# A four-layer graph network on one core: one closing branch, and the order of some loads, sums, turns and copies

## The chip, the core and the metric

The kernel runs on one core of a Trainium2 chip. A core has five engines, each with its own queue that is worked off in order: TensorE (PE, matmuls and transposes; the profile shows the loading of weights beside it as PEld), VectorE (DVE), ScalarE (ACT), GpSimd (POOL) and SyncE (SP), which here issues most of the transfers between the chip's memory (HBM) and the on-chip memory. Engines wait for each other through semaphores. The metric is the device time of the core in microseconds (us); less is better.

## What is computed

The input is x (3327 rows of 256 numbers, float32) and a square matrix adj of 3327 rows. Four layers follow; each normalises x by rows, cuts at zero (h), and adds something to x:

```
# layers 0, 1 and 2
h = relu(layernorm(x));  x = x + adj @ (h @ W0.T + b0)
h = relu(layernorm(x));  x = x + relu(new_adj @ (tanh(h @ Wp + bp) @ Wg) + bg)
#   new_adj: tanh(adj*adj), the 700 largest of each row (all that are positive, if fewer)
h = relu(layernorm(x));  x = x + relu(A_norm @ (h @ W2.T))
#   A_norm: adj + 1, scaled on both sides by 1/sqrt of its row sums
# layer 3
h = relu(layernorm(x));  R = (adj + 1) / row sums;  Xf = Xa = h;  Z = 0
for n in range(2):
    logits = (Xa @ W1.T @ W2.T) @ (Xa @ W3.T).T
    A  = softmax(logits), in each row only the largest up to a mass of 0.9, renormalised
    Xf = R @ Xf;  Xa = A @ Xa
    Z  = Z + Xf @ U1[n].T + Xa @ U2[n].T
x = x + layernorm(h + Z) * ln_g + ln_b
```

The result is x after the four layers, 3327 x 256.

## The kernel before

**Tiling.** The 3327 rows are padded to 26 blocks of 128 (T = 26 in the code, H = 13 the half). All products are in float32. A large product of 26 x 26 blocks is split in 2 x 2 quarters and done with seven products of quarters instead of eight, with sums of quarters made by VectorE. So the blocks are worked off in pairs p and p + 13, and one pair takes 91 matmuls of 128 x 128 with 128 columns, each of which is two records in the profile.

**Layers 0 to 2** (`layers_0_to_2`). `products` (L592) goes over the 13 pairs of a layer; a `Feed` loads the pieces of adj on SP, VectorE and ScalarE make the sums of quarters and the tanh. While a pair's products run, the pair before it is finished, and what the next layer needs of its rows is done by a `Pair`: normalise (`normed`, L359), turn by transposes (L391), project. The stages of a Pair are hooked between the products at counts that the table `WHERE` gives, one entry for each number of stages; with two stages it is layer 1, at the 54th and 82nd product of a pair. The very first rows are loaded and worked on by `first_two` (L737), which has no products to lie behind. In `normed`, VectorE makes mean and variance of two blocks, POOL the inverse root (L98 and L100), and VectorE or ScalarE applies it (L379 and L375).

**Layer 3** (`layer_3_in`, L886). It has two steps. For each of the 26 rows of blocks, TensorE makes the logits (L970), ScalarE their exps (L995), and a search on ScalarE and VectorE (`search_steps`, L999 to L1077) finds the row's threshold and zeroes what is below: it begins with ScalarE's L1012 to L1017 and a pass over the whole row on ScalarE (L1028) and VectorE (L1031), and its last pass over the row (L1073) leaves e, the attention before its division. The search runs AHEAD = 3 rows in front. Then TensorE turns e by blocks (L186), ScalarE copies the turned blocks (L189), and TensorE multiplies them with the values (L197). In between, a `PropagatedPair` (L1149) does R @ Xf, in two phases, with slabs of adj or of its sums; the unit matrix is added to a slab's diagonal block by POOL (L1163). A slab is asked for at the first unit that uses it, and its buffers rotate. `combine` (L1136) makes the sums of quarters on VectorE (L1141 to L1144). `AttentionOfFirstStep` has three parts, `turn`, `node` and `values`; `PropagationOfFirstStep` has `scale`, `turn` and `sums`. `finish3` (L1286) ends a row: it loads z (kept from step 1) and x, adds, normalises, and its `store` writes the result.

**What sets the order.** TensorE's order is the program's, written out by hand: generators yield after each unit, and a plan `{unit: [actions]}` tells what is done at which unit (`run`, L127). On the other engines a scheduler sets the order at build time; `tc.high_priority()` moves an operation forward, and `tc.issue_after(op)` keeps it behind another in its queue. SP's and ScalarE's transfers stand in the queues of their engines with the rest.

**The checks.** The search for a threshold can fail to settle for a row, and a layer-1 row can have more than 700 positive entries. Both are counted, and if it happens the rows, or all layers, are done again by slower code. For this the program reads a flag into a register on all engines and branches (`if_failed`, L1414, with the reads and branches at L1418 and L1419): once in the middle of layer 3, between the two steps, once at the end for step 2, and then once more for all layers (L1740). With this data no branch is taken:

```
        if_failed(0, flags0, st0, kT0, redo_first, lambda name: first_e, redo_second_steps_first)
        nc.vector.memset(w[:, 0:1], 0.0)
        only_exp_and_ln()
        ...
        if_failed(1, flags1, st1, kT1, redo_second, ...)
        ...
    with tc.If(loaded[0] > TOPK):
        all_layers(True, lambda: None)
```

Of the kernel before, what the change touches and what calls it, by code (L numbers as in the profile page):

```python
# [11 lines left out]
F32 = mybir.dt.float32  # L12
I32 = mybir.dt.int32
# [9 lines left out]
D = 256  # L23
# [23 lines left out]
def kernel(  # L47
# [92 lines left out]
    last_copied, last_turned, last_exp, last_found, last_scaled = [], [], [], [], []  # L140
# [101 lines left out]
    def add_nodes(kT, ksum, xT, m, name, bank):  # L242


        n = P
        acc = bank(f"pkq_{name}")
        r, col = (0, m) if m < LOW else (DA, m - LOW)
        i = 0 if m < LOW else 1
        for c in range(NC):
            nc.tensor.matmul(  # L250
                acc[:, :n], kq[:, c, i : i + 2].rearrange("p i e -> p (i e)"), xT[:, c, :n],
                start=(c == 0), stop=(c == NC - 1),
            )
        q = DA - r
        real_n = min(n, N - m * P)
        at = slice(m * P, m * P + n)
        with tc.high_priority():
            nc.scalar.activation(
                kT[r : r + DA, col * P : col * P + real_n], acc[r : r + DA, :real_n], AF.Copy,
                accum_out=ksum[r : r + DA, m : m + 1],  # L260
            )
            nc.scalar.copy(qT[q : q + DA, at], acc[q : q + DA, :n])
        nc.scalar.dma_start(qT[r : r + DA, at], qT[q : q + DA, at])
# [9 lines left out]
    def layers_0_to_2(again):  # L273
# [83 lines left out]
        roots = []  # L357

        def normed(name, x2, dst, split=False):  # L359
# [4 lines left out]
            for i in range(2):  # L364
                nc.vector.bn_stats(st[:, i, :], x2[:, i, :])
                nc.vector.bn_aggr(mv[:, i, :], st[:, i, :])
            with tc.issue_after(roots[-1].ins) if roots else nullcontext():
                roots.append(rsqrt(r, mv[:, :, 1], EPS))
            for i in range(2):
# [8 lines left out]
                else:  # L378
                    nc.vector.tensor_scalar(  # L379
                        dst[:, i, :], x2[:, i, :], mv[:, i, 0:1], r[:, i : i + 1],  # L380
                        ALU.subtract, ALU.mult,
                    )
# [205 lines left out]
        WHERE = {2: (54, 82), 3: (50, 64, 80), 6: (12, 22, 34, 46, 58, 70)}  # L588
# [114 lines left out]
        if not again:  # L703
# [33 lines left out]
            def first_two(product):  # L737

                for a, b in ((0, 1), (1, 2), (2, 4), (4, 6), (6, 9), (9, 12), (12, 13)):
# [11 lines left out]
                    if a == 6:  # L751
                        feed.upto(-1)
                pairs = []
# [121 lines left out]
    def layer_3(again, h3, kT0, ksum0, left, at_end):  # L875
# [3 lines left out]
        with ExitStack() as lctx:  # L879
# [4 lines left out]
            layer_3_in(tag, big, ep, w3, sm3, h3, kT0, ksum0, left, at_end)  # L884

    def layer_3_in(tag, big, ep, w3, sm3, h3, kT0, ksum0, left, at_end):  # L886
# [25 lines left out]
        nc.scalar.dma_start(u1s, u1t.rearrange("s (c p) e -> p s c e", p=P))  # L912
        u2s = big.tile([P, NC, 2, D], F32, name="u2s")
        for i in range(2):
            nc.scalar.dma_start(u2s[:, :, i, :], u2t[i].rearrange("(c p) e -> p c e", p=P))

        gs, bs = u1s[:, 0, 0, :], u1s[:, 0, 1, :]


        halves = big.tile([P, P], F32, name="halves")  # L920
        for i in range(2):
            nc.vector.tensor_tensor(
                halves[:, i * DA : (i + 1) * DA], ident[:, :DA], ident[:, DA:], ALU.add
            )
        ones_sq = big.tile([P, P], F32, name="ones_sq")
        nc.gpsimd.memset(ones_sq, 1.0)

        real = big.tile([P, 1], F32, name="real")
        nc.vector.tensor_scalar(real, ident[:, LAST : LAST + 1], -1.0, 1.0, ALU.mult, ALU.add)
# [206 lines left out]
        def combine(h, ts, a, b):  # L1136
# [7 lines left out]
            nc.vector.tensor_tensor(t3, part(1, 1), part(0, 1), ALU.subtract)  # L1144
# [141 lines left out]
        def finish3(m, y, rows, name):  # L1286
# [3 lines left out]
            nc.sync.dma_start(z, z_dram[:, m, :])  # L1290
            x3 = w3.tile([P, NC, P], F32, tag="hT", name=f"x3_{name}").rearrange("p c n -> p (c n)")
            nc.sync.dma_start(x3, x3_dram[:, m, :])
# [154 lines left out]
        with tc.manual_schedule(engines=PE_ALONE):  # L1447
# [40 lines left out]
            def propagate_first(n, at):  # L1488
# [4 lines left out]
                run(pair.steps(phase), {k * units // T: v for k, v in at.items()})  # L1493
# [41 lines left out]
            for i in range(EARLY):  # L1535
# [4 lines left out]
                if i == 0:  # L1540
                    left.pool, left.bank = (w3, "eT", 3), one_bank
                    propagate_first(0, dict(zip((20, 25), ([what] for what in left.stages))))
# [15 lines left out]
            for m in range(T):  # L1558
# [18 lines left out]
                elif m + 1 < T:  # L1577
                    rows.begin(m + 1)
                    a.turn()
                    left_over = {0: [a.node], 2: [a.values]}  # L1580
# [41 lines left out]
        if_failed(0, flags0, st0, kT0, redo_first, lambda name: first_e, redo_second_steps_first)  # L1622

        nc.vector.memset(w[:, 0:1], 0.0)
        only_exp_and_ln()
        with tc.manual_schedule(engines=PE_ALONE):
# [32 lines left out]
            for i, m in enumerate(ORDER):  # L1661
                ahead = ORDER[i + AHEAD] if i + AHEAD < T else None
                plan, later = passes_apart(1, finder) if ahead else (passes(finder), {})
                if i == 0:
                    p, q = props
                    plan = merged(plan, {2: [p.scale, q.scale], 4: [p.turn], 5: [p.sums, q.turn], 6: [q.sums]})
                acc = rows.finish(m, plan)
                if i == 0:
                    nc.sync.dma_start(gs, ln_g.partition_broadcast(P))
                    nc.sync.dma_start(bs, ln_b.partition_broadcast(P))  # L1670
# [4 lines left out]
                else:  # L1675
                    plan = {4: [lambda: flags1.extend(failed("1", st1))]}
# [5 lines left out]
                if p == 0:  # L1682

                    finish3(m, ys.pop(m), propagate_second(m, plan)[:, :D], f"{m}")()
                else:
# [14 lines left out]
                    else:  # L1700
                        both = pair.whole()
                        for j, k in ((1, m), (0, p)):
                            if pair.last and not j:
                                pair.ended()
                            stores.append(finish3(k, ys.pop(k), both[:, j, :], f"{k}"))
# [4 lines left out]
        def redo_second(m, e, den, name):  # L1710
# [3 lines left out]
        at_end()  # L1714
        spare.append(ep.tile([P, NP], F32, tag="e", name=f"spare{tag}"))
        if_failed(
            1, flags1, st1, kT1, redo_second, lambda name: ep.tile([P, NP], F32, tag="e", name=name), lambda: None
        )


    def all_layers(again, at_end):
        with tc.manual_schedule(engines=PE_ALONE):
            lctx, h3, kT0, ksum0, left = layers_0_to_2(again)
            lctx.close()
            if not again:
# [5 lines left out]
                nc.vector.tensor_copy(flag, most1)  # L1731
        layer_3(again, h3, kT0, ksum0, left, at_end)
# [3 lines left out]
    flag = const.tile([1, 1], I32, name="flag")  # L1736
    loaded = []
    all_layers(False, lambda: loaded.append(nc.values_load(flag[0:1, 0:1])))


    with tc.If(loaded[0] > TOPK):
        all_layers(True, lambda: None)
# [46 lines left out]
```

## Time and profile before

| | us |
|---|---|
| median of three runs | 2549.46 (2548.38 to 2549.57) |
| the profiled execution | 2549.34 |
| its span in the profile | 2547.5 |
| TensorE busy | 2491.6 |
| VectorE busy | 2091.2 |
| ScalarE busy | 1086.9 |
| GpSimd busy | 309.2 |

The span runs from the first to the last record; 1.84 us of the profiled execution lie around it. The layers lie in it like this: layer 0 to about 350 us, layer 1 to 675, layer 2 to 960, step 1 of layer 3 to about 1770, step 2 to 2530, then the last rows' ends and stores. A line of a group names the code's line, the engine, the operation and its tiles. In lines of waits, "PE pt_a L391 <- DVE xn_a L379" is time in which TensorE stood before its transposes of line 391 because VectorE's line 379 had not ended; after it stand the time in all, how often, and the longest. "PEq", "DVEq" and the like are the sequencers of the engines, that is registers, branches and semaphores. The tiles of layer 3's first pass have an a at the end.

### The profile page before, as it was taken

The page shows a single profiled execution, that of the slowest core. Times are in us where ns is not written, and L with a number is a line of the kernel's source. Part 1 is how long each engine was busy: PE and PEld are TensorE (multiplying, and loading weights), DVE is VectorE, ACT ScalarE, POOL GpSimd, SP SyncE. Part 2 cuts the span into 40 slices and gives each one's busy share as a digit, 9 for nine tenths or more (in the row PEclk, how much of TensorE's full clock was granted, in tenths as well). Part 3 has the DMA queues.
Part 4 walks back from the last instruction along what each step waited for, and adds up shares of the span by engine and source line. Part 5 has one row for each costly group of instructions (what it writes and reads, how often), then busy time and mean ns, then how long its engine had stood idle before and what let it go on. Part 6 is the DMA issues. An engine that isn't in the chain of part 4 may idle for free. (4 is left out here: it accounts for less than half of the span.)

```text
span 2547.5 us, 47851 instructions
## 1 busy us (share of the span) xinstructions
PE 2491.6 (98%) x17929; PEld 2255.1 (89%) x17929; DVE 2091.2 (82%) x5538; ACT 1086.9 (43%) x2159; POOL 309.2 (12%) x485
## 2 busy tenths in 40 slices
PE   7999999999999999999999999999999999999997
PEld 7999999999999998888888888887888888888896
DVE  7667788888877778788879797883999999999994
ACT  3110123443111115565656566653555655655551
POOL 2000010000000002000010001000022222222222
PEclk9999999999999999999999999999999999999998
DMA  7677765555797866323232323232433343443342
GB/s 224 187 228 243 226 213 166 182 166 174 246 302 270 273 207 221 108 66 106 73 105 92 108 68 104 69 108 98 161 120 107 113 142 107 127 140 121 107 146 76
DMA packets 181792, 388.46 MB, mean 152 GB/s; under 512 B 19741, under 2 KB 78746, under 8 KB 181530
## 3 DMA queue, kind: packets, MB, share of 16 engines
q1 hardware_dynamic: 153210, 364.31, 44.3%
q10 hardware_dynamic: 28320, 20.80, 2.6%
q8 instruction: 147, 2.41, 0.4%
q14 instruction: 115, 0.94, 0.1%
HBM read 315.44 MB, written 67.89 MB: 150 GB/s over the span
## 5 line engine op out<-in xcount | busy, mean ns | idle before, releaser
L189 ACT COPY eT_a<-pt_a 128x512 f32<-128x512 f32 (+1 forms) x364 | 196.1, 555 | 379.2 <-PE pt_a L186 379.0
L197 PE MATMUL a<-h3a,eT_a 128*128 128x256 f32 x1352 | 323.5, 381 | 0.2 <-ACT eT_a L189 0.2
L197 PE MATMUL a<-vs,eT_a 128*128 128x256 f32 x1352 | 320.4, 381 | 0.2 <-ACT eT_a L189 0.2
L1057 DVE MAX8 cand_a<-w 128x8 f32<-128x128 f32 x1352 | 288.1, 279 | 4.3
L197 PEld LDWEIGHTS a<-h3a,eT_a 128*128 128x128 f32 x1352 | 244.2, 189 | 33.8 <-issue 2.6
L197 PEld LDWEIGHTS a<-vs,eT_a 128*128 128x128 f32 x1352 | 244.7, 190 | 30.3 <-ACT eT_a L189 0.7
L557 PE MATMUL acc_a<-tsa,s_a 128*128 128x128 f32 (+1 forms) x2028 | 268.4, 275 | 0.6 <-DVE tsa L348 0.6
L557 PE MATMUL acc_a<-tsa,a_a 128*128 128x128 f32 x2028 | 250.4, 275 | 2.0 <-DVE tsa L351 2.0
L557 PE MATMUL acc_a<-rhs,a_a 128*128 128x128 f32 (+1 forms) x2028 | 250.7, 276 | 0.2 <-ACT rhs L456 0.2
L557 PEld LDWEIGHTS acc_a<-tsa,s_a 128*128 128x128 f32 x2028 | 247.4, 192 | 1.1 <-DVE tsa L348 0.8
L557 PEld LDWEIGHTS acc_a<-tsa,a_a 128*128 128x128 f32 x2028 | 239.1, 192 | 3.5 <-DVE tsa L351 2.6
L557 PEld LDWEIGHTS acc_a<-rhs,a_a 128*128 128x128 f32 x2028 | 238.4, 192 | 2.3 <-ACT rhs L456 0.4
L1053 DVE SCALAR_TENSOR_TENSOR w<-e_a,t_a 128x896 f32<-128x896 f32 x208 | 226.6, 1090 | 3.0
L995 ACT ACTIVATE e_a<-pl_a 128x1024 f32<-128x1024 f32 x260 | 184.7, 728 | 43.3 <-PE pl_a L970 37.1
L186 PE MATMUL pt_a<-ident,e_a 128*128 128x128 f32 x1352 | 199.5, 273 | 0.2
L1163 POOL TENSOR_TENSOR slab3a<-slab3a,ident 128x128 f32<-128x128 f32 x100 | 92.0, 921 | 861.9 <-DMA slab3a<-in_adj_t_dram 336.1
L1044 DVE SCALAR_TENSOR_TENSOR w<-e_a,t_a 128x3328 uint8<-128x3328 f32 x52 | 192.1, 3695 | 4.3
L1073 DVE SCALAR_TENSOR_TENSOR e_a<-e_a,all_least 128x3328 f32<-128x3328 f32 x52 | 191.9, 3691 | 1.9
L186 PEld LDWEIGHTS pt_a<-ident,e_a 128*128 128x128 f32 x1352 | 166.3, 141 | 29.3 <-ACT eT_a L189 2.6
L395 ACT ACTIVATE xT_a<-pt_a 128x512 f32<-128x512 f32 x52 | 30.8, 593 | 358.3 <-PE pt_a L391 299.6
L688 ACT ACTIVATE a_a<-a_a 128x640 f32<-128x640 f32 (+1 forms) x156 | 101.3, 665 | 169.2 <-DVE a_a L687 149.5
L1194 PE MATMUL f0a<-tsa,slab3a 128*128 128x128 f32 x1352 | 166.5, 277 | 0.0
(246 smaller groups left out, 4248.9 us busy)
## 6 DMA issues: line engine op xcount, KB each, us to landing
slab3a<-s_dram SPq DMA_DIRECT2D x100, 832.0 KB, 4.6
a_a<-in_adj_t_dram SPq DMA_DIRECT2D x312, 256.0 KB, 3.9
slab3a<-in_adj_t_dram SPq DMA_DIRECT2D x79, 832.0 KB, 4.6
a_a<-in_adj_t_dram SPq DMA_DIRECT2D x156, 320.0 KB, 3.8
s_dram<-s_a SPq DMA_DIRECT2D x78, 256.0 KB, 4.6
s_dram<-s_a SPq DMA_DIRECT2D x39, 320.0 KB, 4.6
x_dram<-x_a ACTq DMA_DIRECT2D x39, 256.0 KB, 3.8
s_dram<-a_a SPq DMA_DIRECT2D x26, 256.0 KB, 4.7
```

The source lines that it names most:

```text
L186: nc.tensor.transpose(pt[:, j, :], e[:, k * P : (k + 1) * P], ident)
L189: last_turned.append(nc.scalar.copy(eT[:, : len(blocks), :], pt[:, : len(blocks), :]))
L197: nc.tensor.matmul(acc[:, :width], ready[g][:, j, :], rhs[:, k, :], start=(k == 0), stop=(k == T - 1))
L557: nc.tensor.matmul(self.acc[:, g, at : at + wide], quads[n][:, k - CUTS[c][0], :], t, start=(k == 0 and n in (1, 4)), stop=(k == H - 1 and ...
L688: nc.scalar.activation(a, a, AF.Tanh)
L995: last_exp.append(nc.scalar.activation(dst, src, AF.Exp, accum_out=parts[:, c : c + 1]))
L1044: nc.vector.scalar_tensor_tensor(junk, e, t, e, ALU.is_lt, ALU.mult, accum_out=got)
L1053: nc.vector.scalar_tensor_tensor(w[:, : (b - a) * P], eg, t, eg, ALU.is_lt, ALU.mult, accum_out=below[:, g : g + 1])
L1057: nc.vector.max(cand[:, 8 * k : 8 * k + 8], w[:, (k - a) * P : (k - a + 1) * P])
L1073: nc.vector.scalar_tensor_tensor(e, e, least, e, ALU.is_ge, ALU.mult, accum_out=st["kept"][:, m : m + 1])
L1163: nc.gpsimd.tensor_tensor(x[:, p, :], x[:, p, :], ident, ALU.add)
L1194: nc.tensor.matmul(self.accs[bank][:, c * P : (c + 1) * P], a, self.right(n, k), start=start, stop=last.get(bank) == (n, k), skip_group_ch ...
```

## The change

One check is left, at the very end. VectorE sums up the failures of both steps and layer 1 (`redo`) during the last propagation, and if there are any, all layers are done again in a second pass, which holds the branches of before (`if again:`). The other edits move work:

- `normed` keeps the statistics of a pair, in the first layer's two-engine form, behind the next to last applied normalisation; 12 matmuls of the unit matrix (`busy`) are put at the head of TensorE's queue in `first_two`.
- Layer 1's Pair stages go from units 54 and 82 to 60 and 86.
- At the entry of layer 3 the loads of u1s and u2s on ScalarE's queue come after the last key, `halves` and `real` on VectorE after the last sum of quarters, and the left-over stages of layer 2's last pair go from units 20 and 25 (of 26) to 23 and 25.4, fractions now being allowed.
- In step 1, for the rows that are not interleaved with a propagation, the transposes of the attention (`a.turn`) move into the next row's product, at its group 0, and `node` and `values` to groups 1 and 3.
- In step 2, the turn and sums of the second of two left propagations move from the first row's product to the propagation after it; the loads of ln_g and ln_b go behind that propagation.
- `finish3` of a pair issues its loads of z and x behind the pair's last slab load.

```diff
-            for i in range(2):
-                nc.vector.bn_stats(st[:, i, :], x2[:, i, :])
-                nc.vector.bn_aggr(mv[:, i, :], st[:, i, :])
+            with tc.issue_after(applied[-2].ins) if split and len(applied) > 1 else nullcontext():
+                for i in range(2):
+                    nc.vector.bn_stats(st[:, i, :], x2[:, i, :])
+                    nc.vector.bn_aggr(mv[:, i, :], st[:, i, :])
...
-        WHERE = {2: (54, 82), 3: (50, 64, 80), 6: (12, 22, 34, 46, 58, 70)}
+        WHERE = {2: (60, 86), 3: (50, 64, 80), 6: (12, 22, 34, 46, 58, 70)}
...
+                busy = bank("busy")
+                for _ in range(12):
+                    nc.tensor.matmul(busy[:, :P], ident, ident, start=True, stop=True)
...
+        def constants():
+            nc.scalar.dma_start(u1s, u1t.rearrange("s (c p) e -> p s c e", p=P))
+            for i in range(2):
+                nc.scalar.dma_start(u2s[:, :, i, :], u2t[i].rearrange("(c p) e -> p c e", p=P))
+        def constants_of_vector():
+            for i in range(2):
+                nc.vector.tensor_tensor(halves[:, i * DA : (i + 1) * DA], ident[:, :DA], ident[:, DA:], ALU.add)
+            nc.vector.tensor_scalar(real, ident[:, LAST : LAST + 1], -1.0, 1.0, ALU.mult, ALU.add)
...
-                    propagate_first(0, dict(zip((20, 25), ([what] for what in left.stages))))
+                    propagate_first(0, dict(zip((23, 25.4), ([what] for what in left.stages))))
+                    with tc.issue_after(last_key[-1].ins):
+                        constants()
+                    with tc.issue_after(last_sum[-1].ins):
+                        constants_of_vector()
...
             z = w3.tile([P, D], F32, tag="z", name=f"z1_{name}")
-            nc.sync.dma_start(z, z_dram[:, m, :])
             x3 = w3.tile([P, NC, P], F32, tag="hT", name=f"x3_{name}").rearrange("p c n -> p (c n)")
-            nc.sync.dma_start(x3, x3_dram[:, m, :])
+            with tc.issue_after(behind.ins) if behind else nullcontext():
+                nc.sync.dma_start(z, z_dram[:, m, :])
+                nc.sync.dma_start(x3, x3_dram[:, m, :])
...
-                    a.turn()
-                    left_over = {0: [a.node], 2: [a.values]}
+                    left_over = {0: [a.turn], 1: [a.node], 3: [a.values]}
...
-        if_failed(0, flags0, st0, kT0, redo_first, lambda name: first_e, redo_second_steps_first)
-        nc.vector.memset(w[:, 0:1], 0.0)
-        only_exp_and_ln()
+        if again:
+            if_failed(0, flags0, st0, kT0, redo_first, lambda name: first_e, redo_second_steps_first)
+            nc.vector.memset(w[:, 0:1], 0.0)
+            only_exp_and_ln()
...
-                    plan = merged(plan, {2: [p.scale, q.scale], 4: [p.turn], 5: [p.sums, q.turn], 6: [q.sums]})
+                    plan = merged(plan, {2: [p.scale, q.scale], 5: [p.turn], 6: [p.sums]})
+                    of_next = {3: [q.turn], 12: [q.sums]}
...
-                    plan = {4: [lambda: flags1.extend(failed("1", st1))]}
+                    def last_flags():
+                        flags1.extend(failed("1", st1))
+                        if not again:
+                            nc.vector.scalar_tensor_tensor(
+                                redo, most1, float(TOPK), flags0[LEVELS], ALU.is_gt, ALU.add
+                            )
+                            nc.vector.tensor_tensor(redo, redo, flags1[LEVELS], ALU.add)
+                    plan = {4: [last_flags]}
...
-                            stores.append(finish3(k, ys.pop(k), both[:, j, :], f"{k}"))
+                            stores.append(finish3(k, ys.pop(k), both[:, j, :], f"{k}", pair.loaded))
...
-    all_layers(False, lambda: loaded.append(nc.values_load(flag[0:1, 0:1])))
-    with tc.If(loaded[0] > TOPK):
-        all_layers(True, lambda: None)
+    redo = const.tile([1, 1], F32, name="redo")
+    all_layers(False)
+    n_redo = nc.values_load(redo.bitcast(I32)[0:1, 0:1])
+    with tc.If(n_redo > 0):
+        all_layers(True)
```

## The prediction, made before the changed kernel ran

> **What bounds the kernel now.** I read the page's busy shares first, then TensorE's waits, then busy time by stage, then the order of time around the four largest holes. The page:
>
> ```profile
> PE 2491.6 (98%) x17929; PEld 2255.1 (89%) x17929; DVE 2091.2 (82%) x5538; ACT 1086.9 (43%) x2159; POOL 309.2 (12%) x485
> ```
>
> TensorE (PE) is busy for 2491.6 of 2547.5 us, so all its holes together are 56 us; the diff takes no matmul away that is worth naming, and a gain can come only from those holes, from a cold clock, and from the end. The waits of PE, with total, number and longest, in us:
>
> ```profile
> PE pt_a L391 <- DVE xn_a L379: 16.3, 8, 10.8
> PE f0a L1194 <- PEq L1419: 3.3, 1, 3.3
> PE f1a L1194 <- DMA slab3a<-in_adj_t_dram: 3.0, 1, 3.0
> PE pl_a L970 <- DVEq L1419: 2.5, 1, 2.5
> PE pkq_a L250 <- ACT xT_a L395: 2.2, 1, 2.2
> PE acc_a L557 <- DVE tsa L351: 2.0, 3, 1.4
> PE pt_a L391 <- DVE h3a L420: 1.6, 2, 0.8
> PE pt_f L146 <- ACT eT_a L189: 1.5, 1, 1.5
> PE pt_a L146 <- ACT eT_a L189: 1.5, 6, 0.3
> PE f1a L1194 <- POOL parts_a L990: 1.3, 1, 1.3
> ```
>
> Almost each edit has its line here. The same by stage (window, then its length and the busy time of PE, weight loads, DVE, ACT, POOL, then PE's clock):
>
> ```profile
> 0.00:25.00 25.00, 12.71 (x52) 10.19 (x52) 16.09 (x57) 10.05 (x18) 9.36 (x30) 1.00 0.94 312
> 950.00:975.00 25.00, 21.95 (x165) 19.86 (x165) 16.91 (x34) 8.12 (x24) 7.26 (x15) 0.93 0.69 224
> 1775.00:1800.00 25.00, 22.02 (x152) 19.75 (x154) 20.64 (x61) 10.55 (x25) 1.21 (x5) 0.86 0.50 161
> 2500.00:2525.00 25.00, 22.02 (x135) 20.25 (x134) 6.98 (x14) 4.95 (x9) 5.94 (x7) 0.93 0.47 163
> ```
>
> The start is half empty; the three others are the entry of layer 3, the branch in its middle, and its tail. Which engine would end next is seen at the tail, in order of time (start, us, what):
>
> ```profile
> 2499.22 3.07 PE L1194 MATMUL f1a<-tsa,slab3a 128*128 128x128 f32 x26
> 2501.37 3.69 DVE L1073 SCALAR_TENSOR_TENSOR e_a<-e_a,all_least 128x3328 f32<-128x3328 f32 x1
> 2505.26 0.84 PE L1194 MATMUL f1a<-tsa,slab3a 128*128 128x128 f32 x4 [2.98 <-DMA slab3a<-in_adj_t_dram]
> 2505.89 1.91 PE L186 MATMUL pt_a<-ident,e_a 128*128 128x128 f32 x8
> ```
>
> PE waits 2.98 us for a slab, but its next work, the transposes of the last row's e, needs a DVE pass that ends at 2505.06. VectorE (DVE) is the engine right behind: in the last three rows its pass ends 4.3, 3.1 and 0.8 us before PE takes the row (2449.42 against 2453.68, 2474.45 against 2477.55, 2505.06 against 2505.89).
>
> **What the Trainium skill says.** "Perfetto Trace Analysis", Identifying the Most-Contended Engine, warns that matmul busy time doesn't tell how near TensorE is to its roofline. Here 25.00 busy of 25.00 between 2475 and 2500 stands beside DVE with 22.11, and the passes above show DVE about as late: it agrees. "TensorE: Matmul & The Clock Gate", Part 1, has the clock throttled by default and released by some 3.4 us of activity. The trace agrees: the first 8 transposes take 2.30 us, 8 of the same in step 2 take 1.04. "GPSIMD Engine Reference", 1. Specifications, has GpSimd (POOL) share its SBUF interfaces with VectorE: here POOL's product L1303 takes 0.73 us alone and 3.33 beside the DVE pass at 2501.37. "DMA: Bandwidth & Descriptors", Latency and other measured facts, gives a DMA a fixed cost near 2 us; the last store takes 3.3 from issue to landing.
>
> **The change part by part.** Minus is a gain.
>
> Start (normed L357–380, first matmuls). Before, DVE does the statistics of eight and more blocks before the first normalised block at 10.40, and PE begins at 10.85. In the order of instructions that the changed program has, the first xn stands directly behind the first root, which POOL ends at 6.71: PE could begin near 7.2, 3.6 us earlier, and warm, since 12 matmuls of ident (24 records) run ahead (ident is ready at 2.05). The cold run costs 1.26 on the transposes and 1.9 on the first 8 projections (3.78 against 1.89 later). But DVE is a queue in order: the later blocks now each wait for their own root (0.22 + 0.71 on POOL), and what DVE must do up to the sums tsa (L351), for which PE waited 1.40 at 32.80, is shorter by 0.38 only. I add up tsa at 33.1, after 32.74 before; from there PE has no wait till 78. So 0, between −5.5 (PE's start sets the end, and warm) and +2 (more waits for roots).
>
> Layer 1 (WHERE[2] 54,82 to 60,86). A Pair's turn comes 6 and 4 units later; 6 products of two records at 0.11 are 1.4 us. The waits of PE for xn in 350–675 are 0.5 + 0.4 + 1.8 + 1.3 = 4.0, the longest 1.47. I take −3.5; bounds −4.5 and −2. Nothing new is late: what follows the turn has 5 units still.
>
> Entry of layer 3 (L909–929, L1542). ScalarE's (ACT's) copy xT_a stood at 962.08 behind a DMA issue that waited till 961.60 for the store of x, and DVE's halves waited 1.72 for the same; PE waited 0.71 + 2.22. The constants now come after the keys and after the sums, so ACT's copy is free. But POOL's small memsets still wait for that store till 961.64, with the slab's add L1163 behind them, and pk_mean L936 needs halves, which DVE now makes last: its four combines 1.75 + 1.75 + 2.01 + 1.92 from 958.15 end near 965.7, with 0.51 for halves and real, then 0.3 + 0.15 + 2.19 (mean, kmean, centring) and small gaps: logits near 969.6 where they were at 970.14. −0.5; between −2.9 and +0.5.
>
> Turned attentions (a.turn into the propagation). The six pt_a waits L146 are 1.5 in sum, and the copies now have a unit's time. −1.0; 0 to −1.5.
>
> The branch in the middle, in order of time:
>
> ```profile
> 1774.33 0.29 ACT L1017 ACTIVATE t_a<-mean_a,lnv_a 128x1 f32<-128x1 f32 x1
> ...
> 1778.87 3.07 ACT L1028 ACTIVATE junk_a<-e_a,t_a 128x3328 uint8<-128x3328 f32 x1 [4.25 <-POOLq L1419]
> ...
> 1779.30 3.68 DVE L1031 TENSOR_SCALAR_CACHE_REDUCE w<-e_a,t_a 128x3328 uint8<-128x3328 f32 x1
> ```
>
> All five engines stop at L1419. Without it, ACT's chain L1012–L1017 begins 0.8 earlier (its own wait for the branch was 0.81), t is there at 1773.8, and DVE's pass begins near 1774.2 instead of 1779.30: 5.1. PE had 3.28 + 2.55 of wait, and keeps some of it, as it needs the exps behind ACT's pass. The table load at 1760.85 that goes too was idle time of ACT.
>
> The rest of step 2 hangs on that shift. The queries q.turn/q.sums move out of a stall of 1.55 at 1823, where PE still needs the last copy eT (−0.3 for PE); the row loads z and x3 go behind pair.loaded on SP, which takes away POOL's late add (PE waited 1.27 at 1902) and the slab's wait of 2.98. PE without these holes wants the last e at 2499.22 + 3.07 + 0.84 = 2503.1, less 5.0, 0.3 and 1.3, so 2496.5; DVE, back to back over 2454–2505, has it at 2505.06 − 5.1 = 2500.0. PE's smaller gains in step 2 thus end in one wait for DVE before the last row. What remains: 5.1, plus 0.8 (PE took the row 0.8 after DVE had it), plus 0.5 of the cold clock's cost behind the slab's wait (1.91 − 1.04 + 3.35 − 2.6 = 1.6, most of which a wait of 3.5 for DVE brings back). −6.4; bounds −4 (other row loads late) and −9.5 (DVE gains its waits for POOL's roots too, 0.35 + 1.87 in the last row, and its slowed scan).
>
> End. The last stores are issued until 2537.99, landing is 3.3 later, 2541.3, and the span ends at 2547.5: 6.2 for two checks one after the other and the close. One goes; the two tiny DVE operations for redo lie under the last propagation. The branch above cost 4 to 5 us on a running program; here it may partly lie under the landing. −2; between 0 and −5.
>
> Sum: 0 − 3.5 − 0.5 − 1.0 − 6.4 − 2.0 = −13.4. The profiled execution took 2549.34 (span 2547.5 and 1.84 around it), so 2535.9; the median of the runs is 0.12 above it: 2536.0.
>
> **The rivals.**
> A, the forecast: 2536.0, 0.55. Its own range is 2531 to 2541.
> B, all is delivered: start −4.5, layer 1 −4, entry −2.5, turned −1.5, step 2 −8, end −4: −24.5, 2525. For it: each hole has its edit. Against: DVE's tail and its chain to tsa. 0.2.
> C, other engines hold: only the branch (−5.1) and half of layer 1 (−1.8) come through, 2542.6, as DVE in step 1 and at the entry takes PE's place. For it: DVE has 82% over the whole. Against: in layer 1 its 288 of 325 us leave room. 0.17, a quarter of it less than the measurable.
> D, slower. POOL's add z + y (L1293) waits for z, which SP now asks for only after pair.loaded; it stands in POOL's queue before the next slab's add of ident (L1163), and PE waits for that. One such wait was 1.27. There are 12 pairs: from 13.4 / 12 = 1.1 us a pair on nothing is gained, at 1.6 it is +5.8, 2555. For it: POOL is strictly in order. Against: slabs are asked for earlier and phase 1 leaves some 20 us for 2 loads. 0.04.
> The change not doing what it says: the closing check costs as much alone as with another, and lies in A's range (−11.4).
>
> **How the numbers follow.** What this kernel's measurement can tell from no change is 0.2%, 5.1 us. Faster: A 0.55, B 0.2, three quarters of C 0.13, and 0.03 of the 0.04 that no case holds: 0.91. Same: 0.05, a quarter of C and the other 0.01. Slower: 0.04, D. The range runs from 2525 (B's centre, half of B outside) to 2544, past C's centre.
>
> **What would show it.** The L1419 waits in the middle gone and the pass L1031 directly behind t; xn waits in layer 1 under 1 us; first PE work near 7 but a longer wait for tsa or xn by 33; the slab wait of 2.98 replaced by one for e (L1073) before the last transposes; some 2 us less after the last store. Wrong it would be if PE's first wait-free stretch begins 4 us earlier (B), or if POOL's L1293 waits for z in each pair (D).

## The result, and the profile after

| | us |
|---|---|
| before, 8 runs (the three above among them) | 2551.80 (2548.38 to 2556.44) |
| changed, 8 runs | 2541.06 (2537.56 to 2543.40) |
| ratio changed / before | 0.9956, 95% interval 0.9947 to 0.9965 |
| predicted, beside 2549.46 before | 2536.0, a ratio of 0.9947 |
| span of the profiled execution | 2547.5 before, 2535.7 changed |

The changed kernel is faster by 0.44%, some 11 us. The profiled executions differ by 11.8, the medians by 10.7; the changed kernel's profile is of the fastest of its eight runs. TensorE's waits in the changed kernel (total, number, longest):

```profile
PE prj_a L404 <- ACT xT_a L396: 4.3, 6, 1.3
PE pt_a L392 <- DVE xn_a L380: 3.9, 3, 2.8
PE a L197 <- ACT eT_a L189: 3.5, 9, 1.6
PE pl_a L974 <- ACT e_a L999: 3.0, 1, 3.0
PE f0a L1198 <- POOL slab3a L1167: 2.8, 1, 2.8
PE acc_a L558 <- ACT rhs L437: 2.2, 1, 2.2
...
PE pk_mean_0a L940 <- issue: 1.5, 1, 1.5
...
PE pt_a L186 <- DVE e_a L1077: 1.3, 1, 1.3
```

The waits for the branch, for the last slab and 12.4 of the 16.3 us for xn are gone. But for almost each a new name stands in the list: ScalarE's rhs for xn at the start, xT for xn in layer 1, POOL's slab and `pk_mean` for ScalarE's copy at the entry, ScalarE's exps for the branch, a L197 for the turned attentions, VectorE's e for the slab. Lines are some 1 to 5 higher than before, as the code has shifted. The same four stretches as before (length, then TensorE, weight loads, VectorE, ScalarE, POOL, and TensorE's clock):

```profile
0.00:25.00 25.00, 18.30 (x83) 14.88 (x84) 14.84 (x51) 9.51 (x16) 9.37 (x28) 0.93 0.93 317
950.00:975.00 25.00, 20.54 (x166) 18.21 (x164) 16.84 (x33) 8.24 (x24) 5.68 (x15) 1.00 0.69 224
1775.00:1800.00 25.00, 21.99 (x162) 19.62 (x161) 24.23 (x73) 12.94 (x34) 1.58 (x5) 0.93 0.47 161
2500.00:2525.00 25.00, 24.92 (x176) 23.14 (x173) 4.06 (x17) 4.83 (x9) 3.40 (x6) 1.00 0.23 79
```

TensorE's busy time in the first 25 us rose by 5.6, of which the 24 records of ident are 5.2. It fell at the entry (20.54 after 21.95; there the clock had been 0.93 and is 1.00, and matmuls at half clock count as busy longer), stayed in the middle, and the tail is full. Busy shares don't say what a stage won, so I measured the stages by events that both kernels have, the first or last start of a line:

| stage, from event to event | before | changed | predicted change | change |
|---|---|---|---|---|
| start to the last projection of layer 0 (L403) | 74.4 | 75.7 | 0 | +1.3 |
| to layer 1's last turn (L391, xn) | 600.7 | 600.7 | −3.5 | 0.0 |
| to layer 2's last turn (L391, h3) | 283.6 | 282.2 | 0 | −1.3 |
| entry: to the first logits (L970) | 11.5 | 11.4 | −0.5 | −0.1 |
| step 1: to the first logits of step 2 | 797.0 | 797.2 | −1.0 | +0.2 |
| step 2: to the last product f1a (L1194) | 765.7 | 757.4 | −6.4 | −8.3 |
| to the last store's issue (L1313) | 4.8 | 4.8 | 0 | 0.0 |
| to the end of the span | 9.9 | 6.3 | −2.0 | −3.6 |

Step 2 and the end bring all of it. They are also what holds beyond this one pair of profiles: nine profiles with the changed kernel's code of step 2 took 757.3 to 759.3 there, mean 757.8. The tail, first one line of the kernel before, then the changed kernel in order of time:

```profile
2507.60 3.35 PE L1194 MATMUL f1a<-tsa,slab3a 128*128 128x128 f32 x22
```

```profile
2494.49 3.51 PE L1198 MATMUL f1a<-tsa,slab3a 128*128 128x128 f32 x30
...
2495.43 3.68 DVE L1077 SCALAR_TENSOR_TENSOR e_a<-e_a,all_least 128x3328 f32<-128x3328 f32 x1
...
2499.26 1.06 PE L186 MATMUL pt_a<-ident,e_a 128*128 128x128 f32 x8 [1.26 <-DVE e_a L1077]
...
2500.16 2.62 PE L1198 MATMUL f1a<-tsa,slab3a 128*128 128x128 f32 x22
```

The 26 and 4 records that the slab's wait divided before now run as 30, and TensorE waits 1.26 for VectorE's e in its place. The row is turned at 2499.26, 6.6 earlier; the 8 transposes take 1.06 after 1.91, the 22 records behind them 2.62 after 3.35, as the clock stayed up (1.00 in 2500 to 2525, where it was 0.93): 1.6 more, 8.2 in all.

### The profile page after: what moved, and what is told of

The parts are those of the page before. It is cut to its first block, busy times and chain, and to the rows that moved or that the text cites. A ratio compares the mean times of both kernels' runs of the same rounds, so it can differ in the third digit from the quotient of the medians.

```text
span 2535.7 us, 47811 instructions
## 1 busy us (share of the span) xinstructions
PE 2493.2 (98%) x17953; PEld 2256.4 (89%) x17953; DVE 2087.1 (82%) x5538; ACT 1085.0 (43%) x2158; POOL 302.1 (12%) x485
## 5 line engine op out<-in xcount | busy, mean ns | idle before, releaser
L197 PE MATMUL a<-h3a,eT_a 128*128 128x256 f32 x1352 | 324.1, 381 | 1.7 <-ACT eT_a L189 1.7
L197 PE MATMUL a<-vs,eT_a 128*128 128x256 f32 x1352 | 320.4, 381 | 1.8 <-ACT eT_a L189 1.8
L197 PEld LDWEIGHTS a<-h3a,eT_a 128*128 128x128 f32 x1352 | 244.0, 189 | 35.7 <-ACT eT_a L189 3.4
L197 PEld LDWEIGHTS a<-vs,eT_a 128*128 128x128 f32 x1352 | 244.7, 190 | 32.1 <-ACT eT_a L189 2.5
L1077 DVE SCALAR_TENSOR_TENSOR e_a<-e_a,all_least 128x3328 f32<-128x3328 f32 x52 | 191.6, 3685 | 1.8
```

The source lines that it names most:

```text
L197: nc.tensor.matmul(acc[:, :width], ready[g][:, j, :], rhs[:, k, :], start=(k == 0), stop=(k == T - 1))
L1077: nc.vector.scalar_tensor_tensor(e, e, least, e, ALU.is_ge, ALU.mult, accum_out=st["kept"][:, m : m + 1])
```

## The experiments

All are changes of the changed kernel, except b1. Times of stages are read as in the table above, from one profile of each kernel; all but the last two kernels ran once. What a stage varies by of itself is taken from the other profiles that have the same code in it. No run undoes alone the entry's edits, the turned attentions, the queries and the ln_g and ln_b loads of step 2, or the matmuls of ident.

**e1: the first loads' order.** The statistics are free again, the matmuls of ident stay.

```diff
-            with tc.issue_after(applied[-2].ins) if split and len(applied) > 1 else nullcontext():
-                for i in range(2):
+            for i in range(2):
...
```

> The changed kernel with the statistics of the first blocks free again (normed as before), the 12 matmuls of ident kept. In the changed kernel the last projection of layer 0 starts at 75.7 where it was 74.4 before, a loss of 1.3; in layer 2 that is gone (last products at 944.1 in both). Theory: the loss is the order of VectorE, one wait of 0.9 for a root per pair of blocks, not the matmuls of ident; so the last projection comes back to 74.4 or up to 0.5 earlier, and since VectorE in layer 2 goes by the arrival of adj and not by TensorE, the last product of layer 2 stays at 944.1 within 0.3 and the span is that of the changed kernel within 0.5 (2535.7). Rival 1: the matmuls of ident cause the loss; 75.7 stays. Rival 2: the lead is kept through layer 2; last product at 942.8 and a span 1.3 shorter.

Measured: the last projection at 77.8, later still, and the last product of layer 2 (acc_a) comes 2.4 later than in the changed kernel. TensorE's order of time in this kernel:

```profile
2.10 4.43 PE L755 MATMUL busy<-ident 128*128 128x128 f32 x24 [2.10 <-POOL ident masks.py:199]
11.08 2.30 PE L391 MATMUL pt_a<-ident,xn_a 128*128 128x128 f32 x8 [4.55 <-DVE xn_a L379]
...
33.23 1.65 PE L557 MATMUL acc_a<-tsa,a_a 128*128 128x128 f32 x6 [1.43 <-DVE tsa L351]
34.67 3.62 PE L403 MATMUL prj_a<-w0s,xT_a 128*128 128x256 f32 x8
```

The matmuls of ident end at 6.5, TensorE then stands for 4.55 us, and the first transposes take 2.30, as cold as without them. The sums tsa hold TensorE till 33.23, where it was 32.80 before and 34.06 in the changed kernel. So what the order costs there is about 0.8, less than the 1.3 that my theory put on it, and this run's 77.8 also has a clock that fell after the wait (3.62 for eight projections that take 1.89). My theory missed the number, and so did the two rivals; one profile can't tell the clock from the matmuls of ident. That TensorE takes up these sums as soon as tsa is there is shown in all three (L351 ends at 32.74, 33.18 and 33.89). The loss itself is no accident of one profile: in eleven with the changed start the last projection stands at 75.4 to 76.7, and in the two of before's code at 74.4 and 74.7.

**e3: layer 1's hooks.** `{2: (60, 86)` becomes `{2: (54, 82)`.

> The changed kernel with layer 1's stages at 54 and 82 as before. Theory: the hooks only choose where TensorE meets the lateness of VectorE and ScalarE; the waits of layer 1 were 5.0 in sum before and 5.7 in the changed kernel under other names (xT in place of xn), so here xn waits near 4 come back, xT waits fall below 1.5, and the last turn of layer 1 (676.4 in the changed kernel) moves by less than 0.8. Rival, the prediction's step: the later hooks are worth 3.5, and the turn comes 3.5 later, near 679.9.

Measured: layer 1 takes 602.3, its last turn is at 678.6. TensorE's waits in layer 1 in this kernel, then in the changed one:

```profile
PE pt_a L392 <- DVE xn_a L380: 3.0, 9, 0.5
PE hid_a L444 <- ACT xT_a L396: 0.9, 1, 0.9
PE prj_a L404 <- ACT xT_a L396: 0.7, 2, 0.5
```

```profile
PE prj_a L404 <- ACT xT_a L396: 4.3, 6, 1.3
PE hid_a L444 <- ACT xT_a L396: 0.9, 1, 0.9
PE pt_a L392 <- DVE xn_a L380: 0.4, 1, 0.4
```

The name changes with the hooks, and the sum doesn't fall by them: 4.6 with the old, 5.6 with the new. The turn moved by 2.2, not by less than 0.8 as I had expected, but not by 3.5 either, and nine profiles with the new hooks gave a layer of 598.0 to 602.2 (mean 600.4) against 600.7, 602.3 and 603.4 with the old: some 1.7, no more, and within what one code varies by.

**e12: layer 1 with less work for VectorE.**

```diff
-            nc.vector.scalar_tensor_tensor(a, a, 0.0, a, ALU.max, ALU.mult)
             nc.scalar.activation(a, a, AF.Tanh)
```

> The changed kernel without the positive square before layer 1's tanh (tanh of adj alone is used, so VectorE's 156 operations of 0.67 are left out and layer 1's values differ). Theory: layer 1 goes by VectorE, busy 289 of 325 us and waiting for loads and roots most of the rest; without 100 us of its work TensorE's waits for xT and xn in layer 1 fall from 5 to below 2.5 and the layer, from the last projection of layer 0 to the last turn of layer 1, which took 600.7 in the changed kernel, shortens by 3 to 5. Rival: ScalarE's place in the order or the root on POOL holds TensorE; waits stay at 4 to 6 and the layer within 1.5.

This kernel leaves out the positive square of adj. The other values of layer 1 make the search in layer 3 fail in places, so that all layers run a second time (9098.81 us); only the first 950 us are read. Layer 1 takes 592.6, 8.1 less. Busy time over 350 to 675 us in the changed kernel, then here (TensorE, weight loads, VectorE, ScalarE, POOL):

```profile
350.00:675.00 325.00, 319.34 (x2722) 314.22 (x2721) 289.62 (x554) 123.37 (x214) 22.55 (x29) 1.00 0.57 177
```

```profile
350.00:675.00 325.00, 325.00 (x2788) 321.47 (x2787) 199.34 (x411) 124.35 (x213) 18.55 (x29) 1.00 0.61 183
```

TensorE has no wait left in 325 us. ScalarE's share is the same, so its load did not hold TensorE: VectorE's queue did. The theory holds in this, and more is won than I expected, 8.1 where the waits listed had been 5.6. Two things left that queue together: 90 us of work, and the waits for adj to arrive, which stood before the operation left out (13.6 us of VectorE's time in the changed kernel; here ScalarE waits for adj in its place). This run doesn't part them.

**e14: the same from the other side.** Layer 1's bias is added by `nc.gpsimd` in place of `nc.vector`.

> The changed kernel with layer 1's addition of the bias, 13 operations of 0.69 on VectorE, given to POOL, which is busy 22 of 325 us there. Without 100 us of VectorE's work TensorE's waits in layer 1 went to 0 in e12 and the layer, from the last projection of layer 0 to the last turn of layer 1, took 592.6; in the changed kernel's runs it took 598.0 to 602.2. Theory: VectorE's 9 us, one part of 11 of what e12 left out, lie once in each pair between the products and the next turn; the layer falls to 594 to 598 and TensorE's waits there to under 3. Rival: POOL's slower addition lengthens the chain of each pair and its ports slow VectorE; 600 or more.

Measured: layer 1 takes 605.2, and TensorE waits 7.1 for xT where it waited 4.3. The rival holds. The addition takes 1.65 us on POOL where VectorE took 0.69, and VectorE, with 9 us less to do, now stands 12.8 us in all for its result: work that sits in each pair's chain is not taken off VectorE's queue by giving it to a slower engine.

**e5: the branch in the middle put back.** `if again:` is taken away before `if_failed(0, ...)`, the memset and the table load.

> The changed kernel with the check and branch in the middle of layer 3 put back (with the memset and the table load). Theory: TensorE loses 3.3 at the first row of step 2 (1807.6 to about 1810.8), VectorE's first search pass 5.2 (1774.1 to about 1779.3), and as VectorE has the last row's e ready last, the tail goes by VectorE: last row's turn 2499.3 to 2504.5, span 2535.7 to 2540.9. Rival: TensorE alone sets the end, +3.3, 2539.0. Rival 2, the sum of both waits of TensorE: +5.8 or more.

Measured: step 2 takes 761.9, 4.5 more than in the changed kernel and 2.6 more than the longest of the nine profiles; counted from the first logits of step 2, the last product f0a, just ahead of the first row, comes 4.5 later and the last pass L1077 4.4. Waits of TensorE in step 2:

```profile
PE f0a L1198 <- PEq L1424: 3.3, 1, 3.3
PE pl_a L974 <- DVEq L1424: 2.5, 1, 2.5
...
PE pt_a L186 <- DVE e_a L1077: 1.2, 1, 1.2
```

It lies between the theory (5.2) and the rival (3.3), with the clock at 0.80 in 1775 to 1800 against 0.93. The wait for e stayed at 1.2: TensorE and VectorE are put back by nearly the same, so this run alone can't say which of them carries the loss to the end. The clock has a share in it that this run doesn't give.

**b1: the kernel before without that branch alone.** `if again:` is put before `if_failed(0, ...)`, the memset and the table load; this kernel leaves out the check of step 1.

> The kernel before with the check and branch in the middle of layer 3 alone left out (the check of step 1's search is then missing). Step 2 from its first logits to its last product took 765.7 before and 757.4 in the changed kernel. Theory: TensorE gains 3.3 at the first row, and the late row loads, which hang on TensorE's and POOL's own progress and not on VectorE's lead, keep their 1.5 and their wait at the tail; so 762.4 and no more, within 0.6. Rival: the branch alone brings all of VectorE's 5.2 or more to the end, 760.5 or less.

Measured: step 2 takes 761.5, 4.2 less than before and 0.9 less than the theory, 1.0 more than the rival. The waits for the slab (2.87) and for POOL's late add (1.2) stayed. The turn after the slab's wait:

```profile
2507.19 0.71 PE L1194 MATMUL f1a<-tsa,slab3a 128*128 128x128 f32 x4 [2.87 <-DMA slab3a<-in_adj_t_dram]
2507.74 1.04 PE L186 MATMUL pt_a<-ident,e_a 128*128 128x128 f32 x8
```

Neither the theory (762.4 within 0.6) nor the rival (760.5 or less) is met. The clock didn't fall here after 2.87 us of waiting (1.04 for the 8 transposes). With the 1.6 that a fall cost before, it would have been 763.1, 0.7 above the theory; so the clock can account for the miss, but this run doesn't show that it does. What it shows is that the late row loads keep their two waits without the branch, and that the branch alone brings about half of step 2's gain. In that half is a better clock at the branch's place, 0.93 in 1775 to 1800 after 0.86; the two of the nine profiles of the changed code that had 0.86 there (e1 and e16) took 759.3 and 758.8, 0.8 to 2.0 more than the others. Whether the branch's waits brought the fall is not shown.

**e6: the row loads ahead of the slabs again.** `pair.loaded` is left out of the call of `finish3`.

> The changed kernel with finish3's loads of z and x no longer behind the pair's last slab. Step 2 from its first logits to its last product took 757.4 in the changed kernel and 765.7 before. Theory: POOL's late add at the first pair costs TensorE 1.5 again, and at the tail the slab is asked for only when POOL frees the row's buffer, so the slab lands after e is ready: the last row's turn comes 2.5 later and runs at the cold clock, another 1.6. Together 3 to 5: 760.5 to 762.5. Rival: VectorE sets the tail anyway and hides these loads; under 1, below 758.5.

Measured: step 2 takes 762.3, 4.9 more, within the expected span. TensorE's waits from 1850 on, and the tail:

```profile
PE f1a L1198 <- DMA slab3a<-in_adj_t_dram: 2.6, 1, 2.6
PE f1a L1198 <- POOL parts_a L994: 1.6, 1, 1.6
```

```profile
2505.40 1.22 PE L1198 MATMUL f1a<-tsa,slab3a 128*128 128x128 f32 x4 [2.64 <-DMA slab3a<-in_adj_t_dram]
2506.41 1.91 PE L186 MATMUL pt_a<-ident,e_a 128*128 128x128 f32 x8
```

Both waits are back, and the cold transposes too. The theory holds: VectorE doesn't hide these loads.

**e7: the check for step 2 put back at the end.** `if again:` is taken away before `if_failed(1, ...)`.

> The changed kernel with the check for step 2 put back at the end, so that two checks follow each other there. From the last VectorE operation to the end of the span it was 9.9 before and 6.3 in the changed kernel. Theory: one check in series costs these 3.6; 9.9 again, span 2539.3. Rival (the prediction's lower end): most of a check lies under the landing of the last store; 0 to 2, span below 2537.7, and the 3.6 came from elsewhere.

Measured: step 2 takes 757.3, and from the last VectorE operation (2526.65 and 0.48 long) to the end of the span at 2539.0 it is 11.9. That is 5.6 more than the 6.3 of the changed kernel, where the theory had 3.6 more; that the span came out near the 2539.3 expected is luck, as this run was 2.3 ahead before the tail. From the issue of the last store to the end it was 9.9, 10.5 and 11.9 in the three kernels with two checks there (before, b1, e7), and 5.6 to 7.9, mean 6.7, in ten profiles of kernels with one. The two groups don't overlap, so a second check in series costs, by the means, some 4. The rival, 0 to 2, is out: the landing doesn't hide it.

**e8 and e13: the entry.** In e8 POOL's memsets, collected in a list (not shown), go behind the slabs' additions and `halves` behind two of the four sums.

```diff
-                    with tc.issue_after(last_sum[-1].ins):
+                    with tc.issue_after(last_sum[-2].ins), tc.high_priority():
                         constants_of_vector()
...
+                    with tc.issue_after(added[-1].ins):
+                        for at, value in on_pool:
+                            nc.gpsimd.memset(at, value)
```

> The changed kernel with two more moves at the entry of layer 3: POOL's memsets of constants go behind the additions of the unit matrix to the slabs, and VectorE's halves behind the first two of the four sums of quarters in place of all. From the turn of the last pair (958.7) to the first logits (970.0) it took 11.3 in the changed kernel and 11.4 before, with TensorE waiting 2.8 for POOL's addition and 1.5 for halves. Theory: these two waits hold the entry since ScalarE's copy is free; 11.3 becomes 7.0 to 8.5, and from the first logits of step 1 to those of step 2 it stays at 797.2, so that all of it is kept. Rival: the slabs' arrival or VectorE's sums take their place; above 10.

Measured: 10.4 from the turn to the first logits. The wait for POOL is gone; TensorE waits 2.0 for the keys' sum instead, which stands behind `halves` and a third sum in VectorE's queue. The rival holds. (The clock fell in this run as well, 24 records of f0a take 4.55 where they took 2.92; but the first of VectorE's two centrings of the keys, which the logits need, ended only at 971.5, 8.9 after the turn, so the theory's 8.5 was out of reach at full clock too.) e13 keeps e8's moves and moves the sums too; the last argument of `combine`, new here, chooses the first and third sum or the other two:

```diff
-        FIRST_PHASES = (1, 2, 3), (5, 4, 7, 6)
+        FIRST_PHASES = (1, 2, 3), (5, 7, 4, 6)
...
+            def late_sums():
+                with tc.issue_after(last_centred[-1].ins):
+                    combine(h3, ts, 0, H - 1, (1,))
+                    combine(h3, ts, H - 1, H, (1,))
...
-                    centred = {3: [lambda: centre(kT0, mean0(), "0")]}
+                    centred = {3: [lambda: centre(kT0, mean0(), "0")], 5: [late_sums]}
```

> The entry of layer 3 again, after a look at e8, where the sums and halves put in front of the keys' sum (L944 of the changed kernel, at 967.95 there) left TensorE waiting 2.0 for it: POOL's memsets behind the slabs' additions, only the first and third sum of quarters before halves and the keys' sum, the other two behind the centring of the keys, and the second phase of the first pair in the order 5, 7, 4, 6, so that TensorE uses the early sums first. From the last turn of layer 2 to the first logits it took 11.3 in the changed kernel and 10.4 in e8. Theory: the entry goes by VectorE's queue, and with 3.7 us of sums out of it the logits come 6.0 to 7.5 after the turn and the 797.2 to the first logits of step 2 stay within 0.6: 4 or more won. Rival: the sums moved behind stop TensorE later; the 797.2 grow by what the entry gains. Rival 2: arrival of slab 7 stops TensorE; above 9.

Measured: 7.5, and 797.2 from there to step 2. TensorE before and at the keys' sum, in the changed kernel, then in e13:

```profile
963.59 1.83 PE L1198 MATMUL f0a<-tsa,slab3a 128*128 128x128 f32 x14 [2.81 <-POOL slab3a L1167]
...
966.95 0.35 PE L940 MATMUL pk_mean_0a<-ktotal_0a,halves 128*128 128x1 f32 x2 [1.53 <-issue]
```

```profile
959.61 1.73 PE L1205 MATMUL f0a<-tsa,slab3a 128*128 128x128 f32 x14
962.13 0.35 PE L945 MATMUL pk_mean_0a<-ktotal_0a,halves 128*128 128x1 f32 x2 [0.80 <-PE f0a L1205]
```

4.3 us of waits shrink to 0.8, and step 1 takes no longer for it. The theory holds. (Step 2 took 758.0 in this run, within the 757.3 to 759.3.)

**e16 and e17: the changed kernel and e13's, timed on one chip.**

> The changed kernel itself, on the same chip as the next run. Theory: as measured, a ratio to the kernel before of 0.995 to 0.997. It also gives one more look at layers 0 to 2, whose end (last turn of layer 2) was at 956.6 to 959.9 in the changed kernel's code and at 958.7 and 963.4 in the code of before.

> The kernel of e13, timed. Theory: 3.8 us of the entry are kept to the end, 0.15%: a ratio to the kernel before lower than that of the changed kernel on the same chip by 0.001 to 0.002, 0.993 to 0.995. Rival: VectorE's lead at the tail, 1.3 in the changed kernel's profile, eats it; the same ratio within 0.0005.

Measured: the changed kernel 2538.78 (5 runs), ratio to before 0.9950, interval 0.9936 to 0.9963; e17 2537.76 (5 runs), ratio 0.9940, interval 0.9927 to 0.9954; before 2553.41. In e17's profile the entry took 7.5 and step 2 757.5. The gain over the changed kernel, 0.0010 in the ratios, is some 2.6 us, less than the 3.8 that the stage tells, and the two intervals overlap: e17 beats before, and that it beats the changed kernel is shown in the stage and not by the times. So e17's theory and its rival stay open.

## Why the prediction was right, and where it was off

The forecast was 13.4 us less, and 11.8 came in the profiles (a ratio of 0.9947 foretold, 0.9956 measured; put on the 2549.46 of the forecast it is 2538.2, inside the forecast's own 2531 to 2541). The causes were right where the gain came from: the branch and the row loads in step 2, and the check at the end. How the gain of step 2 reaches the tail was not. That the sum came so near is in good part luck: the start, layer 1, the entry and the turned attentions fell 6.4 short of their terms together, and layer 2, step 2 and the end brought 4.8 more than theirs. More than a quarter of the forecast, layer 1's term, didn't come.

- **Start, 0.** The mechanism was right: TensorE began on xn at 7.35 where it had been 10.85, on a warm clock (the first 8 records of projections took 1.99 after 3.78), and VectorE's chain to tsa ate it. The size was 0.8 short: L351 ended at 33.9, not at 33.1. Three pairs of blocks between 23 and 28 us each wait 0.90 for their own root, as the first line of them shows:

```profile
23.03 0.41 DVE L380 TENSOR_SCALAR xn_a<-rhs,mv_a,r_a 128x256 f32<-128x256 f32 x1 [0.90 <-POOL r_a L100]
```

- **Layer 1, −3.5.** The step that failed is "Nothing new is late: what follows the turn has 5 units still". The projection that follows was late: 4.3 us of waits for xT where 3.9 for xn had been. (The shift of six products, 12 records at 0.11, is 1.3 us and not 1.4.) The prediction itself had 288 of 325 us for VectorE, and took the rest as room when it argued against rival C; e12 shows that VectorE's queue was the bound. By the means of all profiles the hooks bring 1.7 at most.
- **Layer 2.** It gave 1.3 in the profile, which no step foresaw. Eight profiles with the changed kernel's code of layers 0 to 2 ended at 956.6 to 962.6, mean 959.3, and the two of before's at 958.7 and 963.4. So whether start and hooks together gained or lost stays open.
- **Entry, −0.5.** The order held as written: ScalarE's copy came free (at 958.97 in place of 962.08), and the additions behind POOL's memsets and `halves` took its place; 0.1 came, and that was not the edits' doing. The kernel before ran part of its entry at half clock (0.93 over 950 to 975 is 3.4 us at half), which the forecast didn't set apart. b1 has the same entry and ran it at full clock. The matmuls behind ScalarE's copy in before, in b1 and in the changed kernel:

```profile
962.73 1.97 PE L250 MATMUL pkq_a<-xT_a,kq 128*128 128x128 f32 x8 [2.22 <-ACT xT_a L395]
967.09 1.16 PE L250 MATMUL pkq_a<-xT_a,kq 128*128 128x128 f32 x8 [1.87 <-ACT xT_a L395]
959.66 1.11 PE L250 MATMUL pkq_a<-xT_a,kq 128*128 128x128 f32 x8
```

  b1's entry took 10.8, with a store of x that landed 0.35 sooner, and the changed kernel's 11.4 in all five profiles at full clock. So at equal clock the entry's edits brought nothing, and by an estimate from that one profile of b1 they lost 0.2 to 0.5 (11.4 against 10.8 and 10.8 + 0.35). e13 shows that POOL's memsets and `halves`, with VectorE's sums, were the bound.
- **Turned attentions, −1.0.** That term is zero. The wait only moved: before, pt_a L146 waited 1.5 in six parts in step 1; now a L197 waits 1.7 in seven for the same kind of copy.
- **Middle and step 2, −6.4.** The events came as worked out: the pass L1035 began at 1774.10 (1774.2 was foretold), TensorE then waited 3.0 for the exps behind ScalarE's pass, and at the tail VectorE's e took the slab's place. In order of time:

```profile
1774.07 3.07 ACT L1032 ACTIVATE junk_a<-e_a,t_a 128x3328 uint8<-128x3328 f32 x1
1774.10 3.68 DVE L1035 TENSOR_SCALAR_CACHE_REDUCE w<-e_a,t_a 128x3328 uint8<-128x3328 f32 x1 [0.30 <-ACT t_a L1021]
...
1778.29 0.67 PE L974 MATMUL pl_a<-kT_1a,qT 64*128 64x128 f32 x4 [3.01 <-ACT e_a L999]
```

  TensorE had won 3.3 of the foretold 5.0 at the first row and 4.7 from the fourth on (the late add's 1.5), so it met VectorE's e with a wait of 1.26 and not 3.5, and the clock stayed up. The term that was most mis-sized is the clock behind the slab's wait: 0.5 was put down, 1.6 came. The rest is VectorE's last e, which came 6.0 earlier where 5.1 was put down, and here the reason failed. The forecast had VectorE work back to back and carried the 5.1 of its first pass unchanged to the last row. Counted from the first logits of step 2:

| us | before | b1 | e6 | changed |
|---|---|---|---|---|
| first pass over the row (L1031, L1035) begins | 12.2 | 6.9 | 6.9 | 6.9 |
| last pass (L1073, L1077) begins | 734.3 | 731.6 | 730.6 | 728.2 |
| TensorE turns the row before the last | 710.5 | 708.0 | 707.4 | 705.6 |

  Without the branch alone (b1) the first pass is 5.3 earlier and the last only 2.7, about as much as TensorE's rows (some 2.4); and the row loads alone (e6) put the last pass back by 2.4, TensorE's rows by 1.8. So VectorE's lead from the branch doesn't last: in these kernels its last e moves with TensorE's rows, by which link is not shown, and the row loads, whose worth the forecast let end in a wait for VectorE, move it too. That 5.1 was near 6.0 is luck. e6 and b1 show that row loads and branch each bring about half (4.9 and 4.2).
- **End, −2.** The mechanism was right, the size too small: the price of the branch in the middle, "4 to 5 us", nearly held at the end too, 3.6 in the profile and some 4 by the means of all profiles. The forecast let part of it lie under the store's landing; e7 speaks against that. (Its landing is 0.4 late: the 3.3 count from the start of the last issue at 2537.60, which gives 2540.9.)
- **The rivals.** D, POOL's adds behind late rows, didn't come: in the changed kernel TensorE has no wait for POOL in step 2. B failed at the start, the entry and layer 1, though it was nearest on step 2 (8) and the end (4). C was near on layer 1 (half of the term; 1.7 by the means) and the entry, and wrong on step 2 and the end.

## What to carry to other kernels

A wait that ends last on the busiest engine tells where two engines meet, not which of them is late: before crediting its removal, add up the other engine's queue over the stage, and if that is nine tenths full, as VectorE's in layer 1, moving the meeting point may only rename the wait, as it did here. A move that takes a wait away paid where the work behind it was only blocked in a queue and the next engine in line moved with it (the row loads ahead of a slab, 4.9 us); where another engine was as late (the memsets ahead of an addition, e8), it paid once that engine was relieved too (e13). A check on a register that stands behind the last store cost its price in full. And before a small gain is credited to an edit, the clock in that stage is to be compared: the entry's 0.1 was the clock's.

## What was not expected of the hardware

- Whether a wait of nearly 3 us lets the clock fall can't be told from its length: after waits of 2.98, 2.87 and 2.64 us ahead of the same transposes, 8 of them took 1.91, 1.04 and 1.91 (before, b1, e6). The Trainium skill, "TensorE: Matmul & The Clock Gate", Part 1, says that the window in which activity is counted runs freely; these three agree with that. Such a fall cost 1.6 us at the tail, and 2.2 to 2.5 at the entry (13.6, 13.6 and 13.9 in e3, e6 and e14, where the same code took 11.4 at full clock): as much as most edits here.
- Layers 0 to 2, in which loads of adj come in all the time, end at times that differ by 6 us among eight profiles of one code, while step 1 took 797.0 to 797.4 in all profiles but e14's (797.7). One profile is enough for a stage of the second kind, and far from enough for a term of 1 us in the first.
